# Layer 2 of a four-layer convolution kernel: the last 64 channels are split by column couples over the two partition halves, and the projection takes them as two 64-row products

## The chip, the cores and the metric

The kernel runs on one core of one Trainium2 chip. The metric is the device time of one execution in microseconds (us). The time before is the median of three executions; one further execution was taken with the hardware profiler, and all rows below come from that one.

## The reference, cut to what matters

A batch of 32 images with 96 channels of 56x56 goes through four layers. Each layer adds to x a function of the group-normalised x. Layers 0, 1 and 3 are other convolutions (an inverted bottleneck with squeeze-excitation, a wavelet convolution, a 9x9 depthwise convolution) and the change does not touch them. Layer 2 is a quantised inverted bottleneck:

```python
h = bn(conv(x, quant_w(w1), b1, 1, 0, 1), g1, be1, m1, v1)      # 96 -> 576 channels, 1x1
h = act_q(h)                                                    # clip to 0..1, round to 15 steps
h = bn(conv(h, quant_w(w2), b2, 1, 1, HID), g2, be2, m2, v2)    # 576 channels, each 3x3
h = act_q(h)
h = bn(conv(h, quant_w(w3), b3, 1, 0, 1), g3, be3, m3, v3)      # 576 -> 96 channels, 1x1
return x + h
```

## The kernel before, in words

The four layers run one after the other; images or channels stay in DRAM between them. Layer 2 (`layer2`, L1132) works image by image. An image is 3136 pixels, in eight tiles of 392 (NT). One PSUM buffer (`bank`, L1174) holds two tiles of 392 fp32 columns in two PSUM banks, and four such buffers are used in turn.

The 576 hidden channels are five blocks (NBLK): four of 128 channels, and a last one, CC = 4, of 64. The last block's 64 channels are computed twice by the expansion, once for partitions 0 to 63 and once for 64 to 127, so that its depthwise input `apad[4]` holds both copies.

- `expand` (e, L1264): for a block k and a pair of tiles i, four products of the 96-row image (a high and a low part, for two tiles) with 128 columns of weights, then an eviction to int16 by ScalarE or, for a few, VectorE (L1260, L1262).
- `activate` (m, L1283): VectorE clips the block into the padded bf16 picture `apad`, whose rows have 57 elements (PITCH).
- `depthwise` (a, L1294): nine taps, each a product with a diagonal matrix. `quarter` (L1286) issues one such product with 64 rows and 64 columns of weights and 392 pixels, L1291. Four of these, on the four combinations of partition halves, stand next to each other in the program. For k < 4 two PSUM buffers take eight tiles' halves; for the last block one buffer takes four tiles for each half image h, and output half c of the partitions holds tiles 4h+2c and 4h+2c+1, seven picture rows each.
- The depthwise eviction (L1262) reorders pixels: a picture row's columns are stored in four phases (column number modulo 4), NPH = 4. With the last block's two halves holding different picture rows, a group of 392 stored pixels has the first 7 rows on one partition half and the next 7 on the other, of the same phases.
- `activate2` (n, L1322): VectorE clips the stored values in place.
- `project` (j, L1329): for each of four pairs of tiles i and for both tiles j of the pair, five products with 96 columns of weights (L1334). Four are those of the 128-channel blocks. The fifth takes the last block. Since its pixels of one tile lie on one partition half and the other half holds pixels of another tile, the weights `w3` have two versions for it, `w3[:, 8]` with zeros in rows 64 to 127 and `w3[:, 9]` with zeros in rows 0 to 63. The product runs over all 128 rows and half of its weights are zero.
- `add` (d, L1337): VectorE adds each tile to the image (L1341).

The order of the work is written out by hand: `run_steps` walks `L2_ORDER`, in which a letter is a step, digits its arguments, and + and - the next and the previous image. TensorE, VectorE and ScalarE execute exactly in this order; SyncE's queue of DMAs is ordered by the scheduler.

```python
L2_ORDER = """
    e00 e10 e11 e12 l3 j0- d0- e01 e20 e02 e21 r u+ e03 e13 j1- m0 e22 d1- e30 m1 e40 v+ j2- d2- e31
    e41 e23 b+ e42 j3- x+ e32 e33 m2 d3- m3 s++ e43 h0+ m4 a00 a10 o- a11 n1 a01 a20 h1+ a30 a21 l0+
    a31 n0 a40 l1+ n2 l2+ a41 n3 n4
"""
```

So each projection but those of the last image stands between expansions of the next image: the products before it and after it on TensorE are L1272 (or, before j2, the small L1205).

Other places that the prediction reads: `level2` of layer 1 (L920 with 112 rows of data, then L921 with 56 rows), and in layer 0 `filtered` (L493), `expand_phases` (L449) and `project` (L548), whose data are taken through `phases`, two neighbouring fp32 elements of every four.

## Time and profile before

| what | us |
|---|---|
| median of three executions | 5716.87 (5713.84 to 5730.83) |
| the profiled execution | 5714.57 |
| its span, first to last instruction | 5712.6 |
| layer 2 within the span, first expansion to last projection | 3581.7 to 5263.6 |
| ScalarE, VectorE busy in the whole span | 4174.0, 4692.3 |
| TensorE products of L1291 in layer 2 | 20736 |
| TensorE products of L1272 in layer 2 | 2560 |
| TensorE products of L1334 in layer 2 | 1280, of which 256 of the last block |

In rows of the profile PE is TensorE's products and PEld its weight loads, DVE is VectorE, ACT is ScalarE. A row of the timeline gives the start, the duration, the engine, the line, the operation, output<-inputs, rows\*columns of the weights, rows x columns of the data, and how many alike were merged into it. Products overlap: the duration of one is about twice the time until the next one starts, so the time that a product takes on the engine is read from one start to the next.

### The profile page before, as it was taken

To read this page: it belongs to the slowest core of one execution; us is meant where nothing else is said; L and a number is where in the kernel's file an instruction comes from. 1 tells how busy PE (TensorE), PEld (TensorE's weight loads), DVE (VectorE), ACT (ScalarE), POOL (GpSimd) and SP (SyncE) were. 2 spreads that over 40 slices of the span, in tenths; PEclk is the share of its full clock that TensorE was granted. 3 is DMA by queue.
4 is the path that set the end of the run, shared out by engine and by line. 5 is a ranking of instruction groups with operands and counts; after the bars stand their busy time and mean duration, and the time that the engine had idled before them with its cause. 6 is when DMAs were issued, how large, how long until landed. Compare 5 with 4: busy or idle time off the path is not lost.

```text
span 5712.6 us, 137352 instructions
## 1 busy us (share of the span) xinstructions
PE 5494.4 (96%) x59704; PEld 3068.1 (54%) x59704; DVE 4692.3 (82%) x5413; ACT 4174.0 (73%) x6024; POOL 240.6 (4%) x158
## 2 busy tenths in 40 slices
PE   5999999999999999997999999899999999998999
PEld 2333333343343333333566665777788777776444
DVE  6999999999999999997776665777777777775777
ACT  5888888888888888884556654777777777676455
POOL 5000000000000000000000000000000000000000
PEclk9999999999999999998999999999999999999999
DMA  3123333332222332214577666479588796763888
GB/s 99 16 56 61 60 59 58 57 58 44 53 53 59 62 56 55 51 22 60 145 152 150 149 147 123 21 53 51 40 55 46 49 53 40 51 47 38 236 249 247
DMA packets 1285740, 454.45 MB, mean 80 GB/s; under 512 B 1102977, under 2 KB 1281081, under 8 KB 1283217
## 3 DMA queue, kind: packets, MB, share of 16 engines
q1 hardware_dynamic: 1285137, 445.68, 50.1%
q8 instruction: 468, 7.67, 0.6%
q14 instruction: 135, 1.11, 0.1%
HBM read 283.77 MB, written 214.08 MB: 87 GB/s over the span
## 4 chain that ended last, share of the span: by engine, by line
PE 81%; DMA 6%; ACT 4%; DVE 4%; issue 2%; SPq 1%; POOL 1%; ACTq 0%; DVEq 0%; POOLq 0%
PE psd L493 17%; PE psd L1291 13%; PE psj L548 10%; PE ps L426 7%; PE pc L932 7%; PE ps L1272 6%; PE pse L449 6%; PE psj L1334 3%; DMA X<-y 3%; PE pc L920 2%; ACT hi L1242 2%; PE pa L894 2%; PE pc L1466 2%; PE pc L910 1%; DMA raw<-tdiff 1%
## 5 line engine op out<-in xcount | busy, mean ns | idle before, releaser
L467 DVE SCALAR_TENSOR_TENSOR h<-hpad,l_wdw,h 128x3136 f32<-128x3136 f32 x512 | 1782.2, 3481 | 9.1
L493 PE MATMUL psd<-plane,filt 128*32 128x392 f32 (+5 forms) x16384 | 1083.6, 485 | 0.0
L1291 PE MATMUL psd<-apad,diag 64*64 64x392 bf16 x20736 | 916.2, 330 | 67.7 <-issue 63.8
L1291 PEld LDWEIGHTS <-diag 64*64 64x64 bf16 x20736 | 687.5, 106 | 291.7 <-issue 117.0
L493 PEld LDWEIGHTS psd<-plane,filt 128*32 128x32 f32 (+1 forms) x16384 | 390.7, 108 | 674.0 <-issue 621.6
L1262 ACT ACTIVATE u<-ps,o,s 128x784 int16<-128x784 f32 x576 | 536.4, 1002 | 163.9 <-PE ps L1272 145.0
L1262 ACT ACTIVATE a<-psd,o,s 128x784 int16<-128x784 f32 x448 | 423.6, 998 | 279.4 <-PE psd L1291 279.4
L748 ACT COPY T<-raw 128x112 f32<-128x112 f32 (+2 forms) x1386 | 445.6, 385 | 221.9 <-DMA raw<-tdiff 164.1
L426 PE MATMUL ps<-xn,l_wboth 96*128 96x392 f32 (+1 forms) x1536 | 465.2, 505 | 23.8 <-ACT xn L408 22.9
L467 DVE SCALAR_TENSOR_TENSOR hc<-hhalf,l_wdw,hc 128x1568 f32<-128x1568 f32 x256 | 473.7, 1850 | 16.1 <-ACT hc L460 9.5
L1272 PE MATMUL ps<-hi,l_w1q 96*128 96x392 f32 x1280 | 463.2, 362 | 6.8 <-DVE u L1260 3.7
L932 PE MATMUL pc<-x,T 128*112 128x416 f32 (+1 forms) x1152 | 447.3, 525 | 5.9 <-DVE x L870 5.9
L1272 PE MATMUL ps<-lo,l_w1q 96*128 96x392 f32 x1280 | 438.3, 342 | 2.9 <-DVE lo L1250 2.9
L1466 PE MATMUL pc<-x,T 128*112 128x416 f32 (+1 forms) x1152 | 419.4, 525 | 15.0 <-DVE x L1459 10.5
L449 PE MATMUL pse<-xn,l_wboth 96*32 96x392 f32 x4096 | 391.9, 501 | 3.6 <-ACT hab L470 3.6
L426 PEld LDWEIGHTS ps<-xn,l_wboth 96*128 96x128 f32 (+1 forms) x1536 | 219.5, 173 | 248.2 <-issue 53.6
L1466 PEld LDWEIGHTS pc<-x,T 128*112 128x112 f32 x1152 | 203.5, 178 | 230.4 <-issue 185.0
L470 ACT ACTIVATE hab<-psd,o,s 128x784 f32<-128x784 f32 x256 | 283.7, 1113 | 58.5 <-PE psd L493 56.1
L436 ACT ACTIVATE hpad<-ps,o,s 128x784 f32<-128x784 f32 x256 | 278.4, 1104 | 49.2 <-PE ps L426 47.8
L548 PE MATMUL psj<-h,wg 128*32 128x392 f32 x3072 | 307.1, 514 | 0.2 <-DVE wg L535 0.2
L548 PE MATMUL psj<-hab,wg 128*32 128x392 f32 x3072 | 304.8, 509 | 0.0
L453 ACT ACTIVATE plane<-pse,o,s 128x784 f32<-128x784 f32 x256 | 255.9, 1000 | 25.0 <-PE pse L449 20.3
(266 smaller groups left out, 7643.5 us busy)
## 6 DMA issues: line engine op xcount, KB each, us to landing
X<-y SPq DMA_DIRECT2D x192, 392.0 KB
y<-xt SPq DMA_DIRECT2D x108, 392.0 KB
y<-y SPq DMA_DIRECT2D x96, 392.0 KB
out_dram<-y SPq DMA_DIRECT2D x96, 392.0 KB
twav<-zwav SPq DMA_DIRECT2D x768, 36.8 KB
y<-kept SPq DMA_DIRECT2D x72, 392.0 KB
xt<-y SPq DMA_DIRECT2D x59, 392.0 KB
xt<-in_x_dram SPq DMA_DIRECT2D x8, 2352.0 KB
```

The lines of the kernel that those rows point to most:

```text
L426: nc.tensor.matmul(ps[p, j, :NT], wexp[:, k * 128 : k * 128 + 128][:, m], im["xn"][:, j, rows, :].rearrange("c h w -> c (h w)"), start=Tru ...
L449: nc.tensor.matmul(ps[f * GC : (f + 1) * GC, half, :NT].rearrange("p (r w) -> p r w", w=W2), wexp[:, c : c + GC], im["xn"][:, f % 2, r0 : ...
L467: nc.vector.scalar_tensor_tensor(h2, taken(im, k, t), wdw[:, k, t : t + 1], h2, ALU.mult, ALU.add)
L470: nc.scalar.activation(view, ps, AF.Silu, bias=bi[1][:, c : c + 1], scale=sc[1][:, c : c + 1], accum_out=accum)
L493: nc.tensor.matmul(ps[at * GC : (at + 1) * GC, r, :NT].rearrange("p (r w) -> p r w", w=W2)[:, r0 - half * n : r1 - half * n, q0:q1], filt[ ...
L548: nc.tensor.matmul(ps[s * GC : (s + 1) * GC, t, :NT].rearrange("c (m r q) -> c r q m", m=2, q=W4), wg[p, k, c * GC : (c + 1) * GC], phases ...
L748: nc.scalar.copy(to.rearrange("x t (p s) -> x t p s", p=NPH), v[:, k])
L932: nc.tensor.matmul(ps[:PH, to], st["T"][j][:, h, k, :], st["x"][:, j, h, of], start=first and n == 0, stop=not first and n == NK - 1)
L1262: nc.scalar.activation(out, ps, AF.Identity, bias=o[:, c : c + 1], scale=s[:, c : c + 1])
L1272: nc.tensor.matmul(ps[:, j, :NT], w1[:, k * 128 : k * 128 + 128], im[part][:, r0 : r0 + RT, :].rearrange("c h w -> c (h w)"), start=(part ...
L1291: nc.tensor.matmul(ps[q, j, :NT].rearrange("p (r w) -> p r w", w=W), diag[p, k, t, :], v, start=(t == 0), stop=(t == 8))
L1466: nc.tensor.matmul(ps[:, :, to], st["T"][:, h, k, :], st["x"][:, h, :, of], start=(n == 0), stop=(n == NK - 1))
```

## The change

The last block is tiled by columns instead of by rows in the depthwise step. `quarter` gets an argument `columns`; with it a product covers 14 picture rows, and of every four neighbouring picture columns only the couple 2c and 2c+1. It is still 392 pixels, but the data are read in couples of bf16 elements, with two left out between couples. Output half c of the partitions then holds column couple c, that is, two of the four phases, for all rows, and the tile pair j of the buffer is the upper or lower 14 rows. The eviction's pattern follows.

In `project` the eight products of the 128-channel blocks come first, for both tiles of the pair. Then come two products with 64 rows each: tile j = 0 takes partitions 0 to 63, tile j = 1 partitions 64 to 127, with the same weights `w3[:, 8]`, which now have no zeros. The version `w3[:, 9]` and the two memsets go.

```diff
-            ("l2_w1", [C, NBLK * 128], F32R), ("l2_w2", [128, NBLK, 9], F32), ("l2_w3", [128, N9 + 1, C], BF16)))
+            ("l2_w1", [C, NBLK * 128], F32R), ("l2_w2", [128, NBLK, 9], F32), ("l2_w3", [128, N9, C], BF16)))
...
-            nc.vector.memset(w3[HALF:, N9 - 1, :], 0.0)
-            nc.vector.memset(w3[:HALF, N9, :], 0.0)
...
-    def quarter(ps, k, t, r, c, j, tile):
+    def quarter(ps, k, t, r, c, j, tile, columns=None):
...
-        at = (tile * RT + t // 3) * PITCH + t % 3
-        v = apad[k][p, at : at + RT * PITCH].rearrange("p (r w) -> p r w", w=PITCH)[:, :, 0:W]
-        nc.tensor.matmul(ps[q, j, :NT].rearrange("p (r w) -> p r w", w=W), diag[p, k, t, :], v,
-                         start=(t == 0), stop=(t == 8))
+        rows = RT if columns is None else 2 * RT
+        at = (tile * rows + t // 3) * PITCH + t % 3
+        v = apad[k][p, at : at + rows * PITCH].rearrange("p (r w) -> p r w", w=PITCH)[:, :, 0:W]
+        to = ps[q, j, :NT].rearrange("p (r w) -> p r w", r=rows)
+        if columns is not None:
+            v = v.rearrange("p r (q m) -> p r q m", m=NPH)[:, :, :, 2 * columns : 2 * columns + 2]
+            to = to.rearrange("p r (q m) -> p r q m", m=2)
+        nc.tensor.matmul(to, diag[p, k, t, :], v, start=(t == 0), stop=(t == 8))
...
-                        quarter(ps, k, t, c ^ j, c, j, 4 * h + 2 * c + j)
+                        quarter(ps, k, t, c ^ j, c, j, 2 * h + j, c)
...
-            evict(u[:, 2 * n * NT : 2 * (n + 1) * NT].rearrange("p (m j x) -> p j m x", j=2, m=NPH),
-                  p[:, :, :NT].rearrange("p j (x m) -> p j m x", m=NPH), s2, o2, c, f"a{k}{h}{x}" in L2_ON_DVE)
+            v, of = u[:, 2 * n * NT : 2 * (n + 1) * NT], p[:, :, :NT]
+            if k == CC:
+                v, of = v.rearrange("p (j m x) -> p j m x", j=2, m=2), of.rearrange("p j (x m) -> p j m x", m=2)
+            else:
+                v, of = v.rearrange("p (m j x) -> p j m x", j=2, m=NPH), of.rearrange("p j (x m) -> p j m x", m=NPH)
+            evict(v, of, s2, o2, c, f"a{k}{h}{x}" in L2_ON_DVE)
...
-            for k in range(NBLK):
-                n, c = (2 * i + j, k + CC * (i % 2)) if k < CC else (2 * (i // 2) + j, N9 - 1 + i % 2)
-                nc.tensor.matmul(ps[:C, j, :NT], w3[:, c, :], im["a2"][k][:, n * NT : (n + 1) * NT],
-                                 start=(k == 0), stop=(k == CC))
+            for k in range(CC):
+                n = 2 * i + j
+                nc.tensor.matmul(ps[:C, j, :NT], w3[:, k + CC * (i % 2), :], im["a2"][k][:, n * NT : (n + 1) * NT],
+                                 start=(k == 0), stop=False)
+        for j in range(2):
+            p = slice(j * HALF, (j + 1) * HALF)
+            nc.tensor.matmul(ps[:C, j, :NT], w3[p, N9 - 1, :], im["a2"][CC][p, i * NT : (i + 1) * NT],
+                             start=False, stop=True)
```

The host-side layout of `w3` loses its second copy of the last block accordingly.

More of the change, by code (lines that the diff above doesn't have):

```diff
@@ L1611, in quartered, with crossed @@
         return np.concatenate([v[:, :4], ba[:, None], cc[:, None]], axis=1)
-    def crossed(v, twice=False):
+    def crossed(v):
         v = blocks(v)
@@ L1617, in crossed @@
         cc = np.concatenate([v[:64, 4:], v[:64, 4:]])
-        return np.concatenate([v[:, :4], ba, cc] + [cc] * twice, axis=1)
+        return np.concatenate([v[:, :4], ba, cc], axis=1)
     def columns(names, blocks):
@@ L1673, in layouts @@
         "l2_w2": quartered(a[i2 + "w2"].reshape(MID, 9))[:, [0, 1, 2, 3, 5]],
-        "l2_w3": crossed(a[i2 + "w3"].reshape(C, MID).T, twice=True),
+        "l2_w3": crossed(a[i2 + "w3"].reshape(C, MID).T),
         "l2_mid": columns(
```

## The prediction, made before the result was known

> **What bounds the kernel now.** I read the page first, then the stretch of layer 2 alone, then who waits for whom there, then the chain that ended last, then the timeline around one projection.

> ```profile
> span 5712.6 us, 137352 instructions
> PE 5494.4 (96%) x59704; PEld 3068.1 (54%) x59704; DVE 4692.3 (82%) x5413; ACT 4174.0 (73%) x6024; POOL 240.6 (4%) x158
> ```

> The busy times of engines by stretch (layer 2 alone: PE, PEld, DVE, ACT, POOL, granted clock, DMA share, GB/s):

> ```profile
> 3581.70:5263.60 1681.90, 1606.49 (x24704) 1313.29 (x24704) 1218.91 (x2042) 1216.91 (x1222) 22.43 (x32) 0.99 0.71 45
> ```

> TensorE is busy for 1606 of 1682 us at a granted clock of 0.99; VectorE and ScalarE are at 1219 and 1217 us. The waits of PE in that stretch, longest first, begin with

> ```profile
> PE psd L1291 <- issue: 63.8, 70, 2.0
> ```

> and none of the others is over 3.7 us. So in layer 2 TensorE is behind nothing but itself, save one place, which the chain (start, length, what) shows:

> ```profile
> 4177.89 1.66 PE psj L1334 x10
> 4179.55 0.72 PE ps L1272 x4
> 4180.27 0.03 issue
> 4180.29 1.45 ACT u L1262 x2
> ```

> After the last projection of an image the chain leaves TensorE for ScalarE (evictions, two normalisations, the first depthwise eviction) and comes back some 8 us later. This run of ScalarE starts from an expansion that stands behind the projection on TensorE, so a longer or shorter projection moves it along and nothing absorbs the difference. What happens to TensorE's time in a projection, or in the last block's depthwise, is therefore added to the end 32 times.

> **The change part by part.** The number of products and weight loads is the same: ten in each of 4 x 32 = 128 projections, 72 of the last block's depthwise in each image. One projection and its neighbours, from the timeline of PE:

> ```profile
> 4174.03 0.83 PE L1334 MATMUL psj<-a,l_w3q 128*96 128x392 bf16 x4
> 4174.69 0.33 PE L1334 MATMUL psj<-a2c,l_w3q 128*96 128x392 bf16 x1
> 4174.72 0.48 PE L1272 MATMUL ps<-hi,l_w1q 96*128 96x392 f32 x1
> 4175.03 0.34 PE L1272 MATMUL ps<-lo,l_w1q 96*128 96x392 f32 x1
> 4175.21 0.34 PE L1272 MATMUL ps<-hi,l_w1q 96*128 96x392 f32 x1
> ```

> Read the starts: a projection product takes 4174.69 - 4174.03 = 0.66 over four, 166 ns each (the median of all 1154 such steps in the trace), and an expansion product 179. The first expansion product is recorded early, but by the start of the second nothing is lost: from the first product of a projection to the second L1272 the trace has 1.84 us.

> *The pair.* The two 64-row products use different partition halves and different PSUM banks. L548 in layer 0 has the same form (two row halves, each to its own bank) and its products start 7 ns apart, so I take the two as running side by side: one product's 166 ns saved, 128 x 0.166 = 21 us. That is the gain.

> *The switches.* The trace also shows what it costs to go between products that use all row groups and products on a 64-row half, in three places:

> ```profile
> 3028.24 0.33 PE L920 MATMUL pc<-x,T 112*128 112x192 f32 x1
> 3028.49 0.64 PE L921 MATMUL pc<-c,up 56*128 56x224 f32 x2
> 3029.07 0.81 PE L920 MATMUL pc<-x,T 112*128 112x224 f32 x3
> ...
> 4159.67 0.33 PE L1291 MATMUL psd<-apad,diag 64*64 64x392 bf16 x2
> 4159.93 0.45 PE L1272 MATMUL ps<-hi,l_w1q 96*128 96x392 f32 x1
> 4160.22 0.33 PE L1272 MATMUL ps<-lo,l_w1q 96*128 96x392 f32 x1
> ...
> 4181.34 0.34 PE L1272 MATMUL ps<-lo,l_w1q 96*128 96x392 f32 x1
> 4181.61 0.53 PE L1291 MATMUL psd<-apad,diag 64*64 64x392 bf16 x8
> ```

> By the trace's medians: L920 (112 rows) to L921 (56 rows, 128 columns: the nearest form to the new 64 rows by 96) 256 ns, where two L920 of 192 columns are 162 apart: +94. Back, L921 to L920, 279 against 189 for 224 columns: +90. L1272 to L1291 271 against 179: +92, and L1291 to L1272 259 against 168: +91. The step to a product of 128 to 96 rows, as between L1334 and L1272, shows none of this. Behind each switch the next weights were not loaded ahead: after L1291 the second L1272 starts 293 ns behind the first, not 179: +114. On the way in, the second group of L1291 starts 193 behind the first, not 168: +25 for 64 weight columns; in proportion to columns, an estimate of 38 for 96.

> The sum for one projection, first product to second L1272: seven steps of 166 = 1162 to the eighth full product's start; 166 + 93 to the pair; 38 for its weights; 167 for the pair; 91 for the switch back; 293 to the second L1272. That is 2010 ns against 1840: **+170 ns**, or +21.8 us over 128. The two memsets and the order within a projection change nothing in it. From both sides: if the pair's weights are hidden, +132 ns (16.9 us); if 64 rows by 96 columns cost as much to load as 128 columns of L1272, 114 in place of 38, +246 ns (31.5 us).

> [...] 90 to 94 ns each way and the weight load behind it, and with it the saving is more than spent. I go by the rows.

> *The depthwise of the last block.* 18 groups of four products per image, 576 in all, 168 ns each (the median of four starts of L1291). Their data become couples of bf16, 4 bytes in every 8. No such row is there for bf16. The nearest is L548, which reads couples of fp32, 8 bytes in every 16, against L493, which reads whole rows:

> ```profile
> L493 PE MATMUL psd<-plane,filt 128*32 128x392 f32 x4096 | 391.8, 500 | 0.0
> L548 PE MATMUL psj<-hab,wg 128*32 128x392 f32 x3072 | 304.8, 509 | 0.0
> ```

> 9 ns more; group against group in the trace it is 347 against 329, 18 ns more, part of which may come from L548's scattered PSUM writes, which the new products don't have. [...] From both sides: 0, and 18 x 576 = 10 us. A gain is excluded, since the columns are as many. I take 7 ns, 4 us. [...]

> *At nothing.* The evictions of a2c have median 1003 ns with a stride of four fp32, those of u 1002 with none, so the stride of two does nothing. VectorE's preparation of `w3` (722, 659 ns and two like it over 960 columns, now 864, and two memsets of 98 ns at 2799 to 2802 us) lies beside layer 1's matmuls; uncovered it would give back 0.5 us. Its DMA is a tenth shorter, and a few small prefetches for layer 3 change places with stores in SP's queue within layer 1; SP is in no wait of PE there. No wait is added. The fifth product of tile 0 now stands behind tile 1's, but the add never used the difference:

> ```profile
> 4175.06 1.15 DVE L1341 SCALAR_TENSOR_TENSOR xt<-psj,s,xt 96x392 f32<-96x392 f32 x2 [1.55 <-PE psj L1334]
> ```

> Both adds begin after the whole projection (tile 0's last product started at 4173.86). The projection itself ends about as late as before, 1162 + 259 + 38 + 167 = 1626 against 1660 ns, so adds and the reuse of its PSUM buffer, three expansions later, aren't pressed.

> **Sum.** +21.8 + 4 = +26 us on the profiled execution: 5714.6 to 5740. The median shown, 5716.9, lies 2.3 us higher, so 5742.

> **The rivals.**

> *No switch for the pair.* [...] the saving stands: -21 + 4 = -17 us, 5699. For it speaks that L1334 and L1272 change rows from 128 to 96 freely; against it, L921 with 56 rows and 128 columns pays in both directions, each time. It decides from the point where both switches with their weights cost under 166 ns; the rows say 336. If only one of the two is paid, it is about even, 5715 to 5730.

> *The pair doesn't overlap.* Both products use the same 96 output columns; only L548 speaks for two row halves in that case. Then another +21 us: 5763.

> *The couples read slowly.* Up to +97 us, 5839 at the end; a quarter of it gives 5766.

> **How the numbers follow.** The likeliest, switches paid and pair overlapping, has 0.62 and lies at 5733 to 5751. One switch or a hidden part of it, 5708 to 5733: 0.16. No switch at all, about 5699: 0.10. Pair in series or slow couples, 5752 to 5839: 0.12, half of it below 5768. The range 5708 to 5768 leaves out the no-switch case and the worst of the last. A measurement of this kernel tells 0.3% (17 us) from no change, so slower means over 5734 and faster under 5700: faster 0.10, same 0.18, slower 0.72.

> **What would show it.** In the new profile: between the eighth full product of L1334's successor and the pair about 260 ns, the two 64-row products 4 to 7 ns apart, 259 to the first L1272 and 293 from it to the second; groups of the last block's depthwise at 168 to 186 ns; layer 2 some 25 us longer, everything else unchanged. Wrong would be: 166 ns steps right through a projection (no switch), 330 ns for the pair, or depthwise groups well over 186.

## The result, and the profile after

The changed kernel takes 5760.5 us, the median of six executions, against 5712.4 for the kernel before beside it: a ratio of 1.0082 with a 95% interval of 1.0063 to 1.0101, that is 36 to 58 us more (differences in us are a ratio less one, times the time before; the two medians are 48 us apart). A second measurement of both (run e8 below) gave 1.0069, 1.0050 to 1.0088, that is 29 to 50 us. The forecast was 26 us more. The profiled execution took 5760.54 us, its span is 5758.6. Two executions on record, one of the kernel before (15590 us) and one of e2 (14469 us), were in a slow state and stand in no ratio.

The head of its page:

```profile
span 5758.6 us, 137350 instructions
PE 5533.2 (96%) x59704; PEld 3062.6 (53%) x59704; DVE 4690.7 (81%) x5411; ACT 4175.6 (73%) x6024; POOL 238.6 (4%) x158
```

Only PE's busy time has grown by more than 2 us (by 38.8), with the same number of products. Layer 2 alone, in the columns of the prediction (span of the stretch, PE, PEld, DVE, ACT, POOL, clock, DMA share, GB/s):

```profile
3581.40:5308.00 1726.60, 1645.84 (x24704) 1310.09 (x24704) 1217.46 (x2043) 1219.37 (x1222) 22.42 (x32) 0.99 0.69 44
```

The stretch is 44.7 us longer, 39.4 of them busy PE, at the same granted clock of 0.99; it begins at the same place, 3581 us, so all but about 1 us of the difference of the spans, 46.0, is made here. One projection and what stands behind it, in PE's timeline:

```profile
4034.24 0.99 PE L1340 MATMUL psj<-a,l_w3q 128*96 128x392 bf16 x5
4035.16 0.37 PE L1344 MATMUL psj<-a2c,l_w3q 64*96 64x392 bf16 x2
4035.46 0.45 PE L1270 MATMUL ps<-hi,l_w1q 96*128 96x392 f32 x1
4035.75 0.35 PE L1270 MATMUL ps<-lo,l_w1q 96*128 96x392 f32 x1
4035.93 0.34 PE L1270 MATMUL ps<-hi,l_w1q 96*128 96x392 f32 x1
```

Five full products that start at 4034.24 would reach a sixth at 4035.07; the pair starts at 4035.16, 93 ns later. From there it is 0.30 us to the first expansion product and 0.29 from that to the second. In the kernel before these two steps were 0.03 and 0.31, since the first expansion product was recorded early. And the last block's depthwise in one image, before and after (count; shortest, median and longest duration of a product in ns; first and last start):

```profile
L1291 PE MATMUL psd<-apad,diag x71: 326/328/331, 4156.8 to 4159.7; 64*64 64x392 bf16 x71
```

```profile
L1294 PE MATMUL psd<-apad,diag x71: 346/353/360, 4184.6 to 4187.9; 64*64 64x392 bf16 x71
```

No product of the last block in this image is as short as the longest was before. Over all images a group of four takes 196 ns from start to start (the median), where it took 169.

### The profile page after: what moved, and what is told of

It reads as the page before. It is cut to its first block, busy times and chain, and to the rows that moved or that the text cites. A ratio compares the mean times of both kernels' runs of the same rounds, so it can differ in the third digit from the quotient of the medians.

```text
span 5758.6 us, 137350 instructions
## 1 busy us (share of the span) xinstructions
PE 5533.2 (96%) x59704; PEld 3062.6 (53%) x59704; DVE 4690.7 (81%) x5411; ACT 4175.6 (73%) x6024; POOL 238.6 (4%) x158
## 4 chain that ended last, share of the span: by engine, by line
PE 81%; DMA 7%; ACT 5%; DVE 3%; issue 2%; POOL 1%; SPq 1%; ACTq 0%; DVEq 0%; POOLq 0%
PE psd L493 17%; PE psd L1294 13%; PE psj L548 10%; PE ps L426 7%; PE pc L932 7%; PE ps L1270 7%; PE pse L449 6%; PE psj L1340 3%; DMA X<-y 2%; PE pc L920 2%; ACT hi L1240 2%; DMA raw<-tdiff 2%; PE pa L894 2%; PE pc L1476 1%; ACT u L1260 1%
## 5 line engine op out<-in xcount | busy, mean ns | idle before, releaser
L493 PE MATMUL psd<-plane,filt 128*32 128x392 f32 (+5 forms) x16384 | 1083.5, 485 | 0.0
L1294 PE MATMUL psd<-apad,diag 64*64 64x392 bf16 x20736 | 933.3, 333 | 73.7 <-issue 69.9
L1294 PEld LDWEIGHTS <-diag 64*64 64x64 bf16 x20736 | 705.6, 107 | 294.4 <-issue 119.8
L493 PEld LDWEIGHTS psd<-plane,filt 128*32 128x32 f32 (+1 forms) x16384 | 389.9, 108 | 674.8 <-issue 622.3
L1260 ACT ACTIVATE u<-ps,o,s 128x784 int16<-128x784 f32 x576 | 536.6, 1002 | 186.0 <-PE ps L1270 166.9
L1270 PE MATMUL ps<-hi,l_w1q 96*128 96x392 f32 x1280 | 460.0, 359 | 6.7 <-DVE u L1258 3.7
L1270 PE MATMUL ps<-lo,l_w1q 96*128 96x392 f32 x1280 | 438.9, 343 | 2.9 <-DVE lo L1248 2.9
L449 PE MATMUL pse<-xn,l_wboth 96*32 96x392 f32 x4096 | 391.8, 501 | 3.5 <-ACT hab L470 3.5
L548 PE MATMUL psj<-h,wg 128*32 128x392 f32 x3072 | 307.3, 514 | 0.2 <-DVE wg L535 0.2
L548 PE MATMUL psj<-hab,wg 128*32 128x392 f32 x3072 | 305.2, 510 | 0.0
```

The lines of the kernel that those rows point to most:

```text
L449: nc.tensor.matmul(ps[f * GC : (f + 1) * GC, half, :NT].rearrange("p (r w) -> p r w", w=W2), wexp[:, c : c + GC], im["xn"][:, f % 2, r0 : ...
L493: nc.tensor.matmul(ps[at * GC : (at + 1) * GC, r, :NT].rearrange("p (r w) -> p r w", w=W2)[:, r0 - half * n : r1 - half * n, q0:q1], filt[ ...
L548: nc.tensor.matmul(ps[s * GC : (s + 1) * GC, t, :NT].rearrange("c (m r q) -> c r q m", m=2, q=W4), wg[p, k, c * GC : (c + 1) * GC], phases ...
L1260: nc.scalar.activation(out, ps, AF.Identity, bias=o[:, c : c + 1], scale=s[:, c : c + 1])
L1270: nc.tensor.matmul(ps[:, j, :NT], w1[:, k * 128 : k * 128 + 128], im[part][:, r0 : r0 + RT, :].rearrange("c h w -> c (h w)"), start=(part ...
L1294: nc.tensor.matmul(to, diag[p, k, t, :], v, start=(t == 0), stop=(t == 8))
```

## The experiments

The theory from the first trace: two costs, the switches round each pair (162 ns x 128 = 20.7 us by the trace) and the couples (27 ns x 576 = 15.6 us), 36 us together, and some scatter. The rival: one of the two, or a third thing that they trigger, makes most of the 48 us.

**e1_couples_full.** The couples without the pairs:

```diff
-            for k in range(CC):
...
-            nc.tensor.matmul(ps[:C, j, :NT], w3[p, N9 - 1, :], im["a2"][CC][p, i * NT : (i + 1) * NT],
+            for k in range(NBLK):
+                n, c = (2 * i + j, k + CC * (i % 2)) if k < CC else (i, N9 - 1 + j)
```

with the zeros of `w3[:, 8]` and `w3[:, 9]` as before.

> The new column couples in the depthwise, but the projection takes the last block in full 128-row products with two zero-filled weight versions, as before. So no switch in a projection. Theory (the 48 us are two costs, about 21 us of switches in the projections and about 15 us of couples, 27 ns on each of 576 groups, and the rest is the scatter of single executions): projection 1.84 us, depthwise groups of the last block 196 ns, time 15 us over before (ratio 1.0026), at most 20. Rival (the couples cost little in time and the switches with what they trigger make nearly all of the 48 us): ratio under 1.001. Second rival (the couples also lengthen the stalls of the other depthwise groups): 22 us or more over before (ratio 1.004).

Measured: ratio 1.0021 (1.0013 to 1.0030) over 19 executions, 7 to 17 us, 12 at the ratio itself. A projection is back at 1841 ns to the second expansion product, groups of the last block stay at 196, and the image's products are as slow as in the changed kernel:

```profile
L1296 PE MATMUL psd<-apad,diag x71: 347/354/369, 4158.5 to 4161.9; 64*64 64x392 bf16 x71
```

The couples alone are a loss, of the size that the theory gives. Both rivals (under 1.001, over 1.004) are out.

**e2_rows_pair and e7_rows_pair_again.** The pairs without the couples:

```diff
-                        quarter(ps, k, t, c ^ j, c, j, 2 * h + j, c)
+                        quarter(ps, k, t, c ^ j, c, j, 4 * h + 2 * c + j)
...
-            if k == CC:
+            if False:
```

> The projection of the changed kernel (eight full products, then two 64-row products side by side), but the depthwise of the last block takes whole rows as before and its eviction stores them as before. The 64-row products therefore take pixels of a wrong tile; the amount of work is the same. Theory: 259 ns to the pair, 3 ns within it, 293 to the first expansion product, 286 to the second, as in the changed kernel; depthwise groups 169 ns; time 21 us over before (ratio 1.0037). Rival (the switch drags more behind it): 30 us or more (ratio 1.0053).

Measured: ratio 1.0058 (1.0036 to 1.0080), 21 to 46 us. The trace shows the projection at 2004 ns and groups at 169, as expected, but the time leaned to the rival, on three executions. So the same kernel was run again.

> The same kernel as e2_rows_pair (projection with 64-row pairs, depthwise in whole rows; the pixels of the last block in the projection are wrong ones), again, because its interval of 20 to 46 us over before holds both the 22 us that its trace accounts for and 10 us more. Theory (the switches are all of it): 18 to 26 us over before, ratio 1.0031 to 1.0046. Rival (something else comes with the pairs): 30 us or more, ratio over 1.0052.

Measured: ratio 1.0040 (1.0023 to 1.0056), 13 to 32 us, 23 at the ratio itself. The trace has the same projection (2004.5 ns). The two intervals overlap from 21 to 32; the second lies on the theory's 22 us and doesn't hold the rival's 30 in its middle, though its end does. A small third cost is not excluded by these two alone.

**e8_after_again.** No edit.

> The changed kernel again, on the same chip as the others, for a second trace and a narrower interval. Theory (21 to 22 us of switches, 14 to 15 us of couples, and stalls of TensorE at every 128th product of the depthwise that scatter by some 8 us from execution to execution): 36 to 40 us over before, ratio 1.0063 to 1.0070; stalls between 70 and 100 us as in the other traces. Rival (a third cost of about 10 us): ratio 1.008 or more.

Measured: ratio 1.0069 (1.0050 to 1.0088), 39 us more at the ratio itself (the medians are 43 apart); the interval holds the theory's 36 to 40 and, at its end, the rival. Its trace settles more than its time does. It differs from the first trace of the same kernel by 23.5 us of span (5735.1 against 5758.6), with the same projections (2004 ns) and groups (196). The difference is in the waits of PE, of which the first line in layer 2 was, in the first trace and in this one (us in total, times, longest):

```profile
PE psd L1294 <- issue: 69.9, 63, 3.6
```

```profile
PE psd L1294 <- issue: 48.7, 54, 3.0
```

21.2 of the 23.5 us. The kernel before had 63.8 there, e1 53.7, e2 67.4, e7 60.9, so these waits scatter over some 20 us in all the kernels alike. (The expectation's 70 to 100 us of stalls is another count, of what depthwise groups take beyond their usual distance: by 169.5 ns for the four full blocks that is some 90 us in the kernel before, 98 in the first trace and 81 in this one. The scatter of some 8 us was expected too small.) The start times of each trace, summed over the 32 images, show where the time went, in us:

| trace | depthwise of the four full blocks | of the last block | rest of layer 2 | outside layer 2 | span |
|---|---|---|---|---|---|
| kernel before | 871 | 106 | 705 | 4031 | 5713 |
| changed kernel, first trace | 881 | 119 | 727 | 4032 | 5759 |
| changed kernel, e8 | 863 | 116 | 727 | 4030 | 5735 |
| e1, couples alone | 863 | 117 | 705 | 4032 | 5717 |
| e2, pairs alone | 876 | 104 | 732 | 4035 | 5747 |
| e7, pairs alone | 876 | 101 | 726 | 4025 | 5728 |

The rest of layer 2, where the projections stand, is 22 us longer in both traces of the changed kernel and in e7, and not in e1. The last block is 10 to 13 us longer with the couples and not without them; the kernel before has some 5 us of stops in it that e7 has not. The four full blocks, which no edit touches, go from 863 to 881: 9 us of what the first trace has above the two costs are there. For e2 the waits are not enough: it has 19 us over e7, of which 9 lie outside layer 2 and 6 in the rest, and no run tells why.

**e5_pair_first.** The pair ahead of the full products in each projection, so that the weights behind the switch back are bf16 of 96 columns. The theory takes the switch itself at some 92 ns, as the traces have it, and what follows it as the load of the next weights:

```diff
+            p = slice(j * HALF, (j + 1) * HALF)
+            nc.tensor.matmul(ps[:C, j, :NT], w3[p, N9 - 1, :], im["a2"][CC][p, i * NT : (i + 1) * NT],
+                             start=True, stop=False)
+        for j in range(2):
...
-                                 start=(k == 0), stop=False)
-        for j in range(2):
...
-                             start=False, stop=True)
+                                 start=False, stop=(k == CC - 1))
```

> The changed kernel, but in each projection the two 64-row products come ahead of the eight full ones. The switches stay, two per projection; what changes is whose weights are loaded behind the switch back: the bf16 weights of L1340 (96 columns) and no longer the fp32 weights of the first expansion product. Theory ([...] the load of the next weights, in proportion to them): from the pair to the first full product 293 ns as now, from the first full product to the second 166 + 38 = 204, no gap from the last full product to the expansion beyond the 28 and 321 of the kernel before; a projection with its first expansion step 1930 ns instead of 2004, that is 9.5 us less than the changed kernel. Rival (what follows a switch is a fixed restart of about 110 ns, whatever the weights): 2004 ns again, same time.

Measured: ratio to the kernel before 1.0048 (1.0031 to 1.0065), 27 us at the ratio itself, against 39 for the changed kernel in the same comparison. The intervals of the two overlap, so the trace has to decide. In it there are 293 ns from the pair to the first full product and 203 from that to the second, where 204 was expected (medians):

```profile
4042.54 0.34 PE L1270 MATMUL ps<-lo,l_w1q 96*128 96x392 f32 x1
4042.81 0.37 PE L1339 MATMUL psj<-a2c,l_w3q 64*96 64x392 bf16 x2
4043.11 1.53 PE L1344 MATMUL psj<-a,l_w3q 128*96 128x392 bf16 x8
4044.33 0.48 PE L1270 MATMUL ps<-hi,l_w1q 96*128 96x392 f32 x1
4044.65 0.34 PE L1270 MATMUL ps<-lo,l_w1q 96*128 96x392 f32 x1
```

The last full product and the first expansion overlap as in the kernel before (0.32 us from the first L1270 to the second, which is the early record). The part of an image outside its depthwise is 21.85 us, against 22.15 in the changed kernel and 21.43 before: 0.30 us x 32 = 9.7 us given back, 9.5 expected. A fixed restart of 110 ns is out. What follows a switch goes with the weights loaded there: 37 ns for 96 bf16 columns here (203 against 166), and 107 for 128 fp32 columns in the changed kernel (286 against 179).

**e4_pieces.** Other pieces of a row in the last block, by taps:

```diff
-            v = v.rearrange("p r (q m) -> p r q m", m=NPH)[:, :, :, 2 * columns : 2 * columns + 2]
-            to = to.rearrange("p r (q m) -> p r q m", m=2)
+            m = (1, 4, 28)[t // 3]
+            v = v.rearrange("p r (q m) -> p r q m", m=2 * m)[:, :, :, m * columns : m * columns + m]
+            to = to.rearrange("p r (q m) -> p r q m", m=m)
```

> The changed kernel with other pieces in the last block's depthwise, 392 pixels in each product as before: taps 0 to 2 take every second column (pieces of one element), taps 3 to 5 four of every eight (pieces of four), taps 6 to 8 one half of the row (pieces of 28). The pixels are wrong ones; the projection is that of the changed kernel. A piece of two cost 27 ns per group more than whole rows. If the cost goes by the number of pieces (196 of two against 7 rows): taps 0 to 2 about 55 ns more than 169, taps 3 to 5 about 13, taps 6 to 8 about 1. [...]

Measured, by the start times and durations of the trace (medians of 31 images):

| data of a product, 392 bf16 | group, ns | one product, ns |
|---|---|---|
| 7 whole rows of 56 (kernel before) | 169 | 328 |
| 14 pieces of 28 | 177 to 179 | 337 |
| 14 rows, every second element | 180 to 185 | 340 |
| 14 rows, 4 of every 8 | 194 to 200 | 354 |
| 14 rows, 2 of every 4 (changed kernel) | 191 to 201 | 354 |

The number of pieces doesn't explain it: by it, single elements should be the dearest. Nor does the stretch that is read: single elements, pieces of two and pieces of four all take half the elements of 14 rows, spread over the whole row, and single elements have 340 where the others have 354. About 10 of the 27 ns come with 14 rows in place of 7, and 17 more only where pieces of two or four are taken out. Those two are also the only patterns with three steps (rows, pieces, elements) and not two; e4 doesn't tell this apart, but e9 below does.

**e3_pitch64 and e10_pitch60.** Rows of 64 and of 60 elements in the last block's padded picture. 64 elements are 128 bytes, so a couple's place within 8 bytes, and within 16, depends on its tap's column offset alone; 60 are 120 bytes, so its place within 8 bytes does, and within 16 it alternates from row to row. For e3 the theory is that the place makes no difference, the rival that it is what costs:

```diff
-    apad = padded(cp, nc, NBLK, BF16, "apad")
+    apad = padded(cp, nc, CC, BF16, "apad") + padded(cp, nc, 1, BF16, "apadc", pitch=64)
...
```

> The changed kernel with one difference: the last block's padded picture has rows of 64 elements instead of 57, [...]. Theory [...]: all nine taps at about 196 ns per group, time as the changed kernel within 5 us. Rival [...]: taps with column offset 0 and 2 at 168 to 172 ns, those with offset 1 at 196 or more, mean of the nine near 180, time 8 to 10 us under the changed kernel.

Measured: ratio 1.0077 (1.0060 to 1.0093), no gain on the changed kernel. The groups have a mean of 201 ns. Durations of single products fall into heaps, as one image shows:

```profile
L1299 PE MATMUL psd<-apadc,diag x71: 334/342/428, 4175.3 to 4179.1; 64*64 64x392 bf16 x71
```

Of 2232 products (31 images) 1463 took 330 to 349 ns, 383 took 355 to 364 and 371 over 420. The mean, 356, is near the 354 of rows of 57. Neither the theory (all nine taps alike) nor the rival (8 to 10 us under the changed kernel) held. Sorted by start the heaps show no order of column offset. But the order of starts need not tell the four products of a group apart here (a long one may delay its own successor while the others run on, which was not shown); e9 below tells them apart.

> The changed kernel with picture rows of 60 elements for the last block, an even number and a multiple of four, but not of eight: a couple's place within 8 bytes depends on the tap's column alone, [...]. If a couple that crosses a 4- or 8-byte border is what costs 17 ns: taps with column offset 0 and 2 at 337 to 342 ns duration, offset 1 over 354. If it does not matter: all nine alike, at 350 to 356 as with rows of 57 or at 337 to 342.

Measured: mean 359. Of 2304 products 373 took 410 to 419 ns, and most others 340 to 359. Taken by start order, offset 0 is at 346 for both couples, and the heap at 415 is spread over offset 1 of couple 1 (mean 382), offset 2 of couple 0 (371) and offset 1 of couple 0 (359); this spread may come from the order of starts, as in e3. The heap is about a sixth of the products (384), as many as one couple at one offset has. So a couple's place does matter, but not in the way that the expectation had it.

**e6_one_half and e9_pitch64_one_half.** One column couple after the other, so that two products run at once and no two on the same partitions (e9 has the rows of 64 besides):

```diff
-            for t in range(9):
-                for c in range(2):
+            for c in range(2):
+                for t in range(9):
```

> The changed kernel, but the last block's depthwise runs the nine taps of column couple 0 first and those of couple 1 after them. Only two products then run at once, on different partition halves, instead of four, of which two read the same partitions. It takes about 3 us more per image for that reason (some 95 us in all); what is asked is the duration of one product, 328 ns with whole rows and 354 with couples. If two streams of couples out of the same partitions get in each other's way: 337 to 341 ns, the duration of the pieces of 28 and of one element. If the couples themselves are read more slowly: 352 to 356.

The edit did this only in part. The start times have two products at once for the first 12 and the last 10 of an image, a pair every 195 ns. In between four often start together, since couple 1 sets in while couple 0 still runs; the last block takes 4.8 us per image in place of 3.5, not the 3 us more that were expected. The last ten products of one image:

```profile
L1294 PE MATMUL psd<-apad,diag x10: 347/354/358, 4191.7 to 4192.5; 64*64 64x392 bf16 x10
```

354 ns again, against 328 in whole rows, with no second stream on the same partitions: in rows of 57 the couples are slow to read by themselves.

> Picture rows of 64 elements for the last block, and its two column couples one after the other, so that two products run at once and not four. With four at once and rows of 64 the durations of a product fell in three heaps, 336 to 345, 358 and 423 ns, the same tap in different heaps in different images; with rows of 57 they are 354 throughout, with four or two at once. If the heaps come from two streams out of the same partitions whose rows lie alike: 336 to 345 in nearly all products. If they come from something else (the taps' alignment, writes of other engines): the three heaps again.

Measured: the same three heaps as in e3 (1296 products at 330 to 349, 561 at 355 to 364, 372 over 420). Here, too, the first 12 products of an image (taps 0 to 5 of couple 0) and the last 12 (taps 3 to 8 of couple 1) start two at a time, and there the order of starts does tell which product is which. In one image, 11 products of couple 0, then a pair of couple 1 at column offset 0, at offset 1 and at offset 2:

```profile
L1299 PE MATMUL psd<-apadc,diag x11: 336/336/338, 4583.8 to 4584.7; 64*64 64x392 bf16 x11
L1299 PE MATMUL psd<-apadc,diag x2: 342/342/342, 4588.4 to 4588.4; 64*64 64x392 bf16 x2
L1299 PE MATMUL psd<-apadc,diag x2: 423/424/424, 4588.0 to 4588.0; 64*64 64x392 bf16 x2
L1299 PE MATMUL psd<-apadc,diag x2: 356/356/356, 4588.2 to 4588.2; 64*64 64x392 bf16 x2
```

The medians over 32 images are the same: couple 0 takes 335 to 338 at every offset, couple 1 341, 423 and 357. So the heaps are places of couples in their rows. The counts of e3 fit: couple 1 at offset 1, and again at offset 2, is a sixth of 2232 products, 372, and counted there were 371 over 420 and 383 at 355 to 364. The dear couple begins at the last place of a group of four elements and so lies across a border of 8 bytes, counted from where the padded picture begins. Couple 0 at offset 1 lies across a border of 4 bytes only, at 336. Nor is a third step in the pattern dear in itself: couple 0 has three and is as fast as pieces of 28, 337. The two kernels took 5814 and 5821 us, which says nothing on the question since part of the time they run two products at once and not four.

## Why the prediction was right, and where it was wrong

**TensorE bounds layer 2 and nothing absorbs a change in it: right.** 39.4 of 44.7 us are busy PE, and the rest is within the scatter of the waits. e1 and e7 add up: 12 + 23 = 35, against 39 for both at once. "Behind nothing but itself" left out the 63.8 us of stops in the line that it showed, though: they scatter by some 20 us, and the sum has no term for them (see the last section).

**The pair saves one product: right.** The two 64-row products start 3 ns apart in all 128 projections. The rival "the pair doesn't overlap" is out.

**The switches: right, term by term.** To the pair 259 ns (forecast 166 + 93), pair to first expansion product 293 (38 + 167 + 91 = 296), first to second 286 (293). A projection with its next expansion step went from 1842 to 2004 ns, +162 where +170 was forecast, 20.7 us in place of 21.8. Two of the four rows that gave it were of another layer, fp32 and 56 rows, the others between this layer's own expansions and depthwise; all four carried over to the pair. The switches decided: each way 92 ns or so are lost (259 against 166 to the pair; 293 less 166 for the pair and 37 for its weights, which is 90, on the way back, an estimate with the 37 of e5), with the next weights behind. In the changed kernel's trace the load of a product's weights starts 164 ns ahead of the product within a projection and 176 ahead in the expansions (medians); behind a switch, in either direction, it starts 2 ns ahead. That the pair runs side by side did not decide: it was worth 166 ns against some 330. The rival "no switch" is out, in all 128 projections.

**The couples: wrong in size, and this is the step that failed.** The prediction bounded them by 0 and 18 ns per group and took 7 (4 us). The trace has 27 ns, 15.6 us, a sixth of the 97 us that its rival "the couples read slowly" allowed (168 ns once more in each of 576 groups). By its own sign, groups well over 186 ns, the step is refuted (196). L548 was the nearest row, but it could not show either part of the price. Its data and those of L493's 392-pixel form have no rows in them (by the shapes in the trace, 196 couples in one sequence and one run of 392), so the 10 ns that e4 finds for 14 rows in place of 7 are not in the comparison. And its couples are 8 bytes that begin at multiples of 8, so none lies across the border that e9 finds dear. That its fp32 product also takes twice as long for the same 392 columns (347 against 169 ns per group) may have hidden a delay; this was not tried. Nor does any run show whether part of L548's 18 ns is its scattered PSUM writes, for which the prediction went from 18 to 7; the 7, and the 0 that bounds it below, were the author's estimates and not shown. The share of the elements that is used does not settle the price: it is half for every couple, but couple 0 in rows of 64 takes 336 ns, as pieces of 28 do (337), and couple 1 at offset 1 takes 423.

**The sum.** 20.7 + 15.6 = 36 us by the traces; 36 lies on the lower edge of the first interval (36 to 58) and within the second (29 to 50). What the first result has beyond it, some 10 us, fits the scatter of the stops: in its trace 9 us of it lie in depthwise that the change doesn't touch. For the other executions that is argued and not tried. The time lies within the range given, but above the 5733 to 5751 of the likeliest case. That it still lies inside owes something to luck: the upper end came from half of a rival's chance, and the prediction had no term for the scatter of the stops.

**At nothing: right.** VectorE and ScalarE are as busy in layer 2 as before (1217.5 and 1219.4 us), evictions of the last block have median 1003 ns as before, and layer 2 starts at 3581.4 us against 3581.7.

*What stays open.* In rows of 64 couples are not dear as such (335 to 338 ns for couple 0); the dear one, at 423, lies across a border of 8 bytes. A single element cannot, and e4's single elements are at 340; its pieces of four can, and are at 354. But the place within 8 bytes is not all: couple 1 at offset 2 begins 8 bytes behind couple 0 at offset 0, and takes 357 against 336. Rows of 57, an odd number, begin at all eight places of 16 bytes in turn. If the place within 16 bytes were all, which no run shows, the mean over these would be 364 ns, an estimate from e9's figures and e10's heap (336 three times, 423, 407, which is twice 415 less 423, and 357 three times, of which two are assumed), and the trace has 354. So the account is not complete. What counts beside the place within 8 bytes, why couple 1 at offset 2 costs 20 ns more than couple 0, and why 14 rows cost 10 ns more than 7 was not tried, nor was a kernel in which all couples lie at cheap places.

## What to carry to other kernels

Half-empty products were not worth splitting into row halves one pair at a time: a saved product of 392 columns was 166 ns here, and going to 64 rows and back cost about 330, nearly all of it the wait at each switch (90 to 93 ns) and the next weights (37 and 107 ns), which were not loaded ahead. Before such a change, read a switch's price from places in the trace where the row count already changes in the same way (90 to 94 ns in the three here), and if switches must be, put the product with the lightest weights behind them (10 us here). A layout that makes one step neater can be paid for where its data are read, here with 27 ns on each of 576 groups: compare the read pattern in the same type, with the same rows and the same places of its pieces, not just a similar one.

## What was not expected of the hardware

In the depthwise stretches TensorE stops with no engine or DMA to wait for. The chain that ended last in the changed kernel, in one image (start, length, what):

```profile
4046.41 5.63 PE psd L1294 x105
4052.04 1.41 issue
4053.45 5.62 PE psd L1294 x128
4059.07 0.87 issue
4059.94 5.63 PE psd L1294 x119
4065.57 0.86 issue
```

Every piece is 5.6 us long, about the time of 128 products (32 groups of 169 ns and the end of the last one; the chain counts only some of them). In the start times of the traces most distances between such stops (41 of 44 in this one) are 128 products, or a multiple of it, give or take two; with the weight loads that is 256 instructions. In projections and expansions, where 128 products take over 20 us, these stops don't appear: outside the depthwise only seven starts of expansions, all before 3595 us, and one of a projection, at 5305 us, come over 0.45 us behind the start before. The page counts the packets of instructions (number, MB, share of the DMA engines):

```profile
q8 instruction: 468, 7.67, 0.6%
```
